# Moving the last step of a fused AdaLN-FFN block from VectorE to ScalarE and an accumulating DMA

## The chip, the cores and the metric

The kernel runs on one core of one Trainium2 chip. The metric is the device time of one execution in microseconds (us), lower is better. A core has five engines that matter here: TensorE (PE; its weight loads are shown as PEld) multiplies into PSUM, VectorE (DVE), ScalarE (ACT) and GpSimd (POOL) work elementwise, and SyncE (SP) issues DMAs. Each engine runs its own instructions in the order in which the program gives them. They wait for each other through semaphores.

## The reference

`x` has shape (64, 64, 512) in fp32: 64 samples b, 64 channels c, 512 positions t. Every sample chooses one of 200 matrices by its condition. Then comes a feed-forward block with two linear layers, 512 to 1024 to 512. Ahead of each layer the rows are passed through a Walsh-Hadamard transform (FWHT) and rounded to 8 bits with one scale a row; the weights are rounded to -1, 0, 1 times one scale. The result is added to `x`:

```python
def act_quant(x, bits):
    qb = float(2 ** (bits - 1) - 1)
    scale = qb / jnp.clip(jnp.max(jnp.abs(x), axis=-1, keepdims=True), EPS, None)
    q = jnp.clip(jnp.round(x * scale), -qb, qb) / scale
    return _ste(x, q)
def hbitlinear(x, w, bits):
    xq = act_quant(fwht(x), bits)
    wq = weight_quant(w)
    return jnp.einsum('bsd,fd->bsf', xq, wq)
...
w = weights[conditions]
y = jnp.einsum('bct,bcd->bdt', x, w)          # _L0_cond_ref
h = hbitlinear(y, w_up, ACT_BITS)
h = jnp.square(jax.nn.relu(h))
x = x + hbitlinear(h, w_down, ACT_BITS)
```

## The kernel before, in words

**Tiling.** The 64 samples are cut into 16 blocks of four samples (`NP` = 16), so 256 rows (`TOK`) of the feed-forward block; a half `s` of a block is 128 rows, one per partition. Weights are rounded once, transposed and kept in SBUF as bf16 (`wuT`, `wdT`).

**Stages of a block n.** Each is a helper, one for each engine that takes part:

- `load` (L108, SP) brings x with channels and halves of t on the partitions (`xc`); `gather` (L115) brings the four samples' matrices by four indirect DMAs from GpSimd's queue.
- `xbutterfly` (L196) does the first step of the FWHT on x, on GpSimd in the loop; `wsign` (L208, GpSimd) completes the matrices with a signed copy. `cond_pe` (L215) multiplies them, and `cond_act` (L226, ScalarE) copies the product out of PSUM.
- `h1_pe` (L236) does the rest of the first FWHT by a 128 x 128 Hadamard matrix, `h1_dve` (L246 to L251) takes the rows' maxima and the scales, `h1_act` (L256, L263) rounds, `h1_small` (L269, L271) prepares two factors, `t1` (L276) transposes by two DMAs from SP's queue.
- `up_pe` (L284) is the up-projection in two halves h, `up_act` (L294, L296) the relu and the square.
- `mix` (L196) does three butterfly stages of the second FWHT on VectorE, two instructions each; `h2_pe` (L326) the rest on TensorE, `h2_dve` (L335 to L339) the maxima and scales, `h2_act` (L256) and `t2_act` (L354) the rounding, and L356 the transposes, from SP's queue.
- `out_scale` (L361) makes the scale of the result, `osc`. `down_pe` (L366) is the down-projection of one half into one PSUM bank `po`. `down_dve` (L376) is one VectorE instruction that computes po times osc plus `xr`. `xr` is x once more, in the layout of the result, loaded by `load_residual` (L124, SP, one DMA of 512 KB a block). Then SP stores the half (L379, 256 KB).

**Order.** It is written out by hand in the loop `for k in range(NP + 3)` (L440). One turn works on five blocks at once: `up = k` is projected up, `ah = k + 2` goes through its first FWHT (and `ah + 1` through `cond`), `mx = k - 1` is mixed, `tr = k - 2` goes through its second FWHT, and `dn = k - 3` is projected down and stored. The down-projection thus first runs at k = 3. On every engine, and on SP's and GpSimd's DMA queues, the instructions follow in the order of the loop's text. So SP has in a turn: load of `xc` for block k + 4, load of `xr` for `tr`, the two transposes of `t2_act`, the store of half 0, the two transposes of `t1`, the store of half 1. GpSimd has: two butterflies and `wsign` for `ah + 1`, then four gathers for k + 4. In the last turns the upward stages fall away, and blocks 14 and 15 have their rounding and transposes by halves (L455, L471).

**Buffers.** The six PSUM banks of pool `ps` make three tiles used in turn by cond, h1, up and h2; pool `pso` has two banks for `po`. `xr` has two buffers, the result tile `ot` four of half a block.

Of the kernel before, what the change touches and what calls it, by code (L numbers as in the profile page):

```python
# [7 lines left out]
F32 = mybir.dt.float32  # L8
BF16 = mybir.dt.bfloat16
I32 = mybir.dt.int32  # L10
AF = mybir.ActivationFunctionType
ALU = mybir.AluOpType
# [3 lines left out]
P = 128  # L16
# [22 lines left out]
def adaln_ffn_kernel(  # L39
# [10 lines left out]
    nc = tc.nc  # L50
    B, C, T = x.shape
# [10 lines left out]

    xv = x.rearrange("(n s b) c t -> n (b c) s t", s=2, b=2)
    xcv = x.rearrange("(n b) c (a t) -> n (c a) b t", b=4, a=2)
    ov = out.rearrange("(n s b) c t -> n s (b c) t", s=2, b=2)
    cwv = cw.rearrange("s c d -> (s c) d")

    const = ctx.enter_context(tc.tile_pool(name="const", bufs=1))
# [1 line left out]
    work = ctx.enter_context(tc.tile_pool(name="work", bufs=2))  # L70
# [26 lines left out]
    idx = const.tile([P, B], I32, tag="idx")  # L97
    nc.vector.tensor_scalar(idx, cnd, float(C), row_f, ALU.mult, ALU.add)

    xc, xr, w2 = {}, {}, {}  # L100

    def load_hm():
        nc.sync.dma_start(hm, had)
# [1 line left out]
    def load(n):  # L105

        xc[n] = loads.tile([P, 4, T // 2], F32, tag="xc", name=f"xc_{n}")
        nc.sync.dma_start(xc[n], xcv[n])  # L108

    def gather(n):  # L110

        w2[n] = loads.tile([P, 4, P], F32, tag="w2", name=f"w2_{n}")
        for b in range(4):
            i = 4 * n + b
            nc.gpsimd.indirect_dma_start(  # L115
                out=w2[n][:, b, :D],
                out_offset=None,
                in_=cwv,
                in_offset=bass.IndirectOffsetOnAxis(ap=idx[:, i : i + 1], axis=0),
            )  # L120

    def load_residual(n):
        xr[n] = work.tile([P, 2, T], F32, tag="xr", name=f"xr_{n}")
        nc.sync.dma_start(xr[n], xv[n])  # L124


    wuT = const.tile([P, NJ, FF], BF16, tag="wuT")
# [64 lines left out]
    pz2, qs2, t2, r2, q2T, osc, po, ot = {}, {}, {}, {}, {}, {}, {}, {}  # L192
# [5 lines left out]
    def xbutterfly(n, engine="p"):  # L198

        xb[n] = work.tile([P, 4, 2, P], F32, tag="xb", name=f"xb_{n}")  # L200
        v = xc[n].rearrange("p b (j q) -> p b j q", j=2)
        e = nc.gpsimd if engine == "p" else nc.vector
        for i in range(2):
            butterfly(e, [xb[n][:, :, j] for j in range(2)], [v[:, :, j] for j in range(2)], i)

    def wsign(n):

        nc.gpsimd.tensor_scalar(w2[n][:, :, D:], w2[n][:, :, :D], sgn, 1.0, ALU.mult, ALU.mult)  # L208

    def cond_pe(n):  # L210

        py[n] = ps.tile([P, 4, 2, 2, D], F32, tag="ps", name=f"py_{n}")
        for b in range(4):
            for j in range(2):
                nc.tensor.matmul(  # L215
                    py[n][:, b, j].rearrange("p a d -> p (a d)"),
                    xb[n][:, b, j, :],
                    w2[n][:, b, :],
                    start=True,
                    stop=True,  # L220
                )

    def cond_act(n):

        yT[n] = work.tile([P, 4, 4, D], F32, tag="yT", name=f"yT_{n}")
        nc.scalar.copy(  # L226
            yT[n].rearrange("p c b d -> p b c d"), py[n].rearrange("p b j a d -> p b (j a) d")
        )
# [49 lines left out]
    def up_pe(n, h):  # L278

        ph[h] = ps.tile([P, NF // 2, TOK], F32, tag="ps", name=f"ph_{n}_{h}")  # L280
        for i in range(NF // 2):
            f = h * NF // 2 + i
            for j in range(NJ):
                nc.tensor.matmul(  # L284
                    ph[h][:, i],
                    wuT[:, j, f * P : (f + 1) * P],
                    qT[n][:, j, :],
                    start=(j == 0),
                    stop=(j == NJ - 1),
                )  # L290

    def up_act(n, h):

        nc.scalar.activation(ph[h], ph[h], AF.Relu)  # L294
        gf[n, h] = work.tile([P, NF // 2, TOK], F32, tag="gf", bufs=4, name=f"gf_{n}_{h}")
        nc.scalar.activation(gf[n, h], ph[h], AF.Square)  # L296
# [26 lines left out]
    def h2_pe(n, s):  # L323
        pz2[s] = ps.tile([P, NF, P], F32, tag="ps", name=f"pz2_{n}_{s}")
        for f in range(NF):
            nc.tensor.matmul(  # L326
                pz2[s][:, f, :], mixed[n, 2][:, f, s * P : (s + 1) * P], hm, start=True, stop=True
            )

    def h2_dve(n, s):  # L330
        if s == 0:
            t2[n] = small.tile([P, 2], F32, tag="t2", name=f"t2_{n}")
        am = small.tile([P, 1], F32, tag="am2", name=f"am2_{n}_{s}")
        flat = pz2[s].rearrange("p f q -> p (f q)")
        nc.vector.tensor_reduce(am, flat, AX.X, ALU.max, apply_absolute_value=True)  # L335
        t = t2[n][:, s : s + 1]
        nc.vector.tensor_scalar(t, am, 1.0 / QB, e2[n][:, s : s + 1], ALU.mult, ALU.max)  # L337
        qs2[s] = small.tile([P, 1], F32, tag="qs2", name=f"qs2_{n}_{s}")
        nc.vector.reciprocal(qs2[s], t)  # L339

    def h2_act(n, s):
        if s == 0:
            r2[n] = work.tile([P, 2, FF], F32, tag="r2", bufs=1, name=f"r2_{n}")
        quantize(r2[n][:, s], pz2[s].rearrange("p f q -> p (f q)"), qs2[s])
# [3 lines left out]
    def t2_act(n, s=None):  # L348

        if n not in q2T:  # L350
            q2[n] = work.tile([P, 2, FF], BF16, tag="q2", name=f"q2_{n}")
            q2T[n] = work.tile([P, NF, TOK], BF16, tag="q2T", name=f"q2T_{n}")
        sl = slice(0, 2) if s is None else slice(s, s + 1)
        nc.scalar.activation(q2[n][:, sl], r2[n][:, sl], AF.Copy, bias=-MAGIC)  # L354
        for i in range(2)[sl]:
            nc.sync.dma_start_transpose(q2T[n][:, :, i * P : (i + 1) * P], q2[n][:, i])  # L356
# [14 lines left out]
                stop=(f == NF - 1),  # L371
            )

    def down_dve(n, s):
        o = work.tile([P, T], F32, tag="ot", bufs=4, name=f"ot_{n}_{s}")
        nc.vector.scalar_tensor_tensor(  # L376
            o, po[s], osc[n][:, s : s + 1], xr[n][:, s], ALU.mult, ALU.add
        )
        nc.sync.dma_start(ov[n, s], o)  # L379

    ku = const.tile([P, 1], F32, tag="ku")
    ke = const.tile([P, 1], F32, tag="ke")
# [9 lines left out]
    def valid(n):  # L392
        return 0 <= n < NP
# [46 lines left out]
    for k in range(NP + 3):  # L440
        up, ah, tr, dn, mx = k, k + 2, k - 2, k - 3, k - 1
        if valid(k + 4):
            load(k + 4)
        if valid(tr):
            load_residual(tr)
        if valid(ah + 1):
            xbutterfly(ah + 1)
            wsign(ah + 1)
        if valid(k + 4):
            gather(k + 4)  # L450
        if valid(tr):
            h2_pe(tr, 0)
            h2_dve(tr, 0)
            h2_act(tr, 0)
            if tr >= NP - 2:  # L455
                t2_act(tr, 0)
        if valid(up):
            up_pe(up, 0)
        if valid(mx) and mx < NP - 1:
            mix(mx, 1, 0)  # L460
            mix(mx, 1, 1)
        if valid(up):
            up_act(up, 0)
        if k == 0:
            cond_pe(2)
            cond_act(2)
        if valid(tr):
            h2_pe(tr, 1)
            h2_dve(tr, 1)
            h2_act(tr, 1)  # L470
            if tr >= NP - 2:  # L471
                t2_act(tr, 1)
        if valid(up):
            up_pe(up, 1)
            up_act(up, 1)
        if valid(tr) and tr < NP - 2:
            t2_act(tr)
        if valid(mx) and mx < NP - 1:
            mix(mx, 2, 0)
        if valid(ah):  # L480
            h1_pe(ah)
            h1_dve(ah)
        if valid(mx) and mx < NP - 1:
            mix(mx, 2, 1)
        if mx == NP - 1:
            for s in range(2):
                for stage in (1, 2):
                    mix(mx, stage, 0, s)
                    mix(mx, stage, 1, s)
        if valid(dn):  # L490
            out_scale(dn)
            down_pe(dn, 0)
            down_dve(dn, 0)
        if valid(ah):
            h1_act(ah)
            t1(ah)
            h1_small(ah)
        if valid(up):
            mix(up, 0, 0)
            mix(up, 0, 1)  # L500
        if valid(ah + 1):
            cond_pe(ah + 1)
            cond_act(ah + 1)
        if valid(dn):
            down_pe(dn, 1)
            down_dve(dn, 1)
        if k == 0:
            for i in range(CH):
                weight_sum("down", i, "a")
        if k == 1:  # L510
            sd.append(weight_scale("down"))
            for i in range(2):
                weight_round("down", wdT, i)
                weight_clip("down", wdT, i)
        if k == 2:
            for i in range(2, CH):
                weight_round("down", wdT, i)
                weight_clip("down", wdT, i)
# [29 lines left out]
```

## Time and profile before

| | us |
|---|---|
| median of the three runs shown | 295.7 |
| lowest and highest of them | 294.04 and 297.8 |
| the profiled execution, whole time | 298.29 |
| the profiled execution, span from first to last instruction | 296.5 |
| TensorE busy, mean granted clock 0.954 | 246.7 (83%) |
| VectorE busy | 244.7 (83%) |
| ScalarE busy | 199.8 (67%) |
| GpSimd busy | 126.5 (43%) |
| DMA queue of SP, share of the 16 engines' time | 61.1% |
| DMA queue of GpSimd, share of the 16 engines' time | 3.8% |
| `down_dve`, L376, 32 instructions | 23.7, or 747 ns each |
| rounding from PSUM, L256, 32 of 512 columns | 20.2, or 685 ns each |
| store, issue to landing, 256 KB | 2.4 |
| residual load, issue to landing, 512 KB | 4.0, 5.5, 6.9 (least, median, most) |
| gather, GpSimd's time for one issue | 0.94 to 1.87, median 0.95 |

The profile is of one execution. A group is all instructions of one source line on one engine with the same operands; its busy time is the sum over them. "Idle before" is how long the engine stood still ahead of a group, and the arrow names what ended the wait. In the row of slices the span is cut into 40 equal parts and each digit is the busy share of one in tenths. TensorE's matmuls overlap, so that their start times say more than the busy sum. A DMA's issue on a queue is short; what is told as landing is the time until its data had arrived.

### The profile page before, as it was taken

The numbers are of one execution on the slowest core, as the hardware profiler recorded it, in microseconds if no ns is written. First come the engines' busy times: TensorE is split into PE (matmuls) and PEld (weight loads), VectorE is DVE, ScalarE is ACT, GpSimd is POOL, SyncE is SP. The second block draws the span as 40 slices with busy tenths as digits, with TensorE's granted clock in tenths as the row PEclk, the third lists the DMA queues.
The fourth block names the chain that finished last, engine by engine and source line by source line (L and its number), as shares of the span: only waits on it lengthen the run. The fifth ranks groups of instructions, "written<-read, shape, count | busy, mean of one in ns | idle before, by whom it ended". The sixth has DMA issues, their size and how long they took to land. (4 is left out here: it accounts for less than half of the span.)

```text
span 296.5 us, 4792 instructions
## 1 busy us (share of the span) xinstructions
PE 246.7 (83%) x1796; PEld 203.0 (68%) x1796; DVE 244.7 (83%) x331; ACT 199.8 (67%) x231; POOL 126.5 (43%) x111
## 2 busy tenths in 40 slices
PE   0064969493789999998999999999999998987954
PEld 0063959492767878786878787878887878756721
DVE  1446708879789999999999999999999999999942
ACT  1346186965968686858686868687868786665350
POOL 2787804894653737282809683737310000000000
PEclk9998677988979999999999999999999999999989
DMA  5944594327495867575666766668683748275973
GB/s 193 359 112 92 92 299 108 100 45 143 124 142 162 150 188 156 184 156 182 138 200 127 213 136 201 140 198 137 201 141 109 142 108 177 81 206 112 214 169 143
DMA packets 81206, 46.55 MB, mean 157 GB/s; under 512 B 62112, under 2 KB 70432, under 8 KB 81184
## 3 DMA queue, kind: packets, MB, share of 16 engines
q1 hardware_dynamic: 79136, 44.15, 61.1%
q0 software_dynamic: 2048, 2.10, 3.8%
q8 instruction: 14, 0.23, 0.3%
q14 instruction: 8, 0.07, 0.1%
HBM read 23.17 MB, written 8.39 MB: 106 GB/s over the span
## 5 line engine op out<-in xcount | busy, mean ns | idle before, releaser
L256 ACT ACTIVATE r<-pz,qs 128x512 f32<-128x512 f32 (+1 forms) x64 | 55.8, 899 | 67.6 <-DVE qs L339 47.2
L196 DVE TENSOR_TENSOR g<-g 128x1024 f32<-128x1024 f32 (+1 forms) x68 | 83.6, 1256 | 0.1
L115 POOL DMA_INDIRECT w<-in_L_cond_weights,idx x64 | 71.9, 1123 | 21.9 <-issue 16.6
L284 PE MATMUL ph<-qT,wuT 128*128 128x256 bf16 x512 | 64.4, 282 | 10.4 <-ACT r L256 10.3
L326 PE MATMUL pz<-hm,g 128*128 128x128 f32 x512 | 63.6, 277 | 2.1 <-DVE g L196 2.1
L284 PEld LDWEIGHTS <-wuT 128*128 128x128 bf16 x512 | 51.9, 101 | 19.5 <-issue 12.5
L366 PE MATMUL po<-wdT,q2T 128*128 128x512 bf16 x256 | 60.8, 385 | 5.2 <-DMA q2T<-q 5.2
L326 PEld LDWEIGHTS pz<-hm,g 128*128 128x128 f32 x512 | 61.5, 193 | 4.9 <-DVE g L196 2.3
L196 POOL TENSOR_TENSOR xb<-xc 128x512 f32<-128x512 f32 x26 | 34.6, 1353 | 65.8 <-DMA xc<-in_x 63.6
L366 PEld LDWEIGHTS <-q2T 128*128 128x128 bf16 x256 | 25.2, 99 | 31.3 <-DMA q2T<-q 5.9
L236 PE MATMUL pz<-hm,yT 128*128 128x128 f32 x256 | 36.4, 301 | 8.8 <-ACT yT L226 8.2
L196 DVE TENSOR_TENSOR g<-gf,gf 128x1024 f32<-128x1024 f32 x32 | 41.9, 1349 | 1.6 <-ACT gf L296 1.6
L236 PEld LDWEIGHTS pz<-hm,yT 128*128 128x128 f32 x256 | 33.5, 211 | 12.4 <-ACT yT L226 9.0
L215 PE MATMUL py<-w,xb 128*128 128x128 f32 x256 | 35.5, 298 | 5.1 <-issue 3.8
L215 PEld LDWEIGHTS py<-w,xb 128*128 128x128 f32 x256 | 34.7, 213 | 6.8 <-issue 3.9
L335 DVE TENSOR_REDUCE am<-pz 128x1 f32<-128x1024 f32 x32 | 38.9, 1215 | 0.4 <-PE pz L326 0.4
L296 ACT ACTIVATE gf<-ph 128x1024 f32<-128x1024 f32 x32 | 32.8, 1024 | 1.0
L294 ACT ACTIVATE ph<-ph 128x1024 f32<-128x1024 f32 x32 | 32.5, 1016 | 0.0
L246 DVE TENSOR_REDUCE am<-pz 128x2 f32<-128x1024 f32 x16 | 19.6, 1223 | 15.6 <-PE pz L236 15.6
L354 ACT ACTIVATE q<-r 128x2048 bf16<-128x2048 f32 (+1 forms) x18 | 30.9, 1714 | 0.1
L376 DVE SCALAR_TENSOR_TENSOR ot<-po,osc,xr 128x512 f32<-128x512 f32 x32 | 23.7, 747 | 7.7 <-PE po L366 6.3
L208 POOL TENSOR_SCALAR w<-w,sgn 128x256 f32<-128x256 f32 x16 | 20.1, 1255 | 1.3 <-DMA w<-in_L_cond_weights,idx 1.1
(46 smaller groups left out, 109.6 us busy)
## 6 DMA issues: line engine op xcount, KB each, us to landing
xc<-in_x SPq DMA_DIRECT2D x16, 512.0 KB, 11.0
xr<-in_x SPq DMA_DIRECT2D x16, 512.0 KB, 5.5
out<-ot SPq DMA_DIRECT2D x32, 256.0 KB, 2.4
raw_up<-in_L_ffn_w_up SPq DMA_DIRECT2D x4, 512.0 KB, 7.6
raw_down<-in_L_ffn_w_down SPq DMA_DIRECT2D x4, 512.0 KB
w<-in_L_cond_weights,idx POOLq DMA_INDIRECT x64, 3.6
qT<-q SPq DMA_TRANSPOSE x32, 3.1
q2T<-q SPq DMA_TRANSPOSE x32, 3.2
```

The source lines that it names most:

```text
L115: nc.gpsimd.indirect_dma_start(out=w2[n][:, b, :D], out_offset=None, in_=cwv, in_offset=bass.IndirectOffsetOnAxis(ap=idx[:, i : i + 1], ax ...
L196: engine.tensor_tensor(dst[i], src[0], src[1], (ALU.add, ALU.subtract)[i])
L215: nc.tensor.matmul(py[n][:, b, j].rearrange("p a d -> p (a d)"), xb[n][:, b, j, :], w2[n][:, b, :], start=True, stop=True,)
L236: nc.tensor.matmul(pz1[n][:, s, c * P : (c + 1) * P], y[:, j * 2 + a, s * P : (s + 1) * P], hm, start=True, stop=True,)
L256: nc.scalar.activation(r, pz, AF.Copy, bias=MAGIC, scale=qs)
L284: nc.tensor.matmul(ph[h][:, i], wuT[:, j, f * P : (f + 1) * P], qT[n][:, j, :], start=(j == 0), stop=(j == NJ - 1),)
L294: nc.scalar.activation(ph[h], ph[h], AF.Relu)
L296: nc.scalar.activation(gf[n, h], ph[h], AF.Square)
L326: nc.tensor.matmul(pz2[s][:, f, :], mixed[n, 2][:, f, s * P : (s + 1) * P], hm, start=True, stop=True)
L335: nc.vector.tensor_reduce(am, flat, AX.X, ALU.max, apply_absolute_value=True)
L354: nc.scalar.activation(q2[n][:, sl], r2[n][:, sl], AF.Copy, bias=-MAGIC)
L366: nc.tensor.matmul(po[s], q2T[n][:, f, s * P : (s + 1) * P], wdT[:, f, :], start=(f == 0), stop=(f == NF - 1),)
```

## The change

`down_dve` is replaced by `down_act` and `finish`, and the residual load goes. ScalarE now takes each half's sums from PSUM, multiplies them with `osc` and writes them into a result tile of a whole block (`ot`, two buffers). After both halves a DMA from GpSimd's queue reads x from HBM and adds it onto that tile in SBUF (`accum_op=ALU.add`). SP then stores the block in one DMA of 512 KB, with the layout of `ov` changed to match. `out_scale` stays on VectorE.

```diff
-    ov = out.rearrange("(n s b) c t -> n s (b c) t", s=2, b=2)
+    ov = out.rearrange("(n s b) c t -> n (b c) s t", s=2, b=2)
...
-    def load_residual(n):
-        xr[n] = work.tile([P, 2, T], F32, tag="xr", name=f"xr_{n}")
-        nc.sync.dma_start(xr[n], xv[n])
...
-    def down_dve(n, s):
-        o = work.tile([P, T], F32, tag="ot", bufs=4, name=f"ot_{n}_{s}")
-        nc.vector.scalar_tensor_tensor(
-            o, po[s], osc[n][:, s : s + 1], xr[n][:, s], ALU.mult, ALU.add
-        )
-        nc.sync.dma_start(ov[n, s], o)
+    def down_act(n, s):
+
+        if s == 0:
+            ot[n] = work.tile([P, 2, T], F32, tag="ot", name=f"ot_{n}")
+        nc.scalar.activation(ot[n][:, s], po[s], AF.Copy, scale=osc[n][:, s : s + 1])
+
+    def finish(n, s=None):
+
+        sl = slice(0, 2) if s is None else slice(s, s + 1)
+        nc.gpsimd.dma_start(ot[n][:, sl], xv[n][:, sl], accum_op=ALU.add)
+        nc.sync.dma_start(ov[n][:, sl], ot[n][:, sl])
...
-        if valid(tr):
-            load_residual(tr)
...
             down_pe(dn, 0)
-            down_dve(dn, 0)
+            down_act(dn, 0)
...
             down_pe(dn, 1)
-            down_dve(dn, 1)
+            down_act(dn, 1)
+            finish(dn)
```

In the loop the first half's step stands between `down_pe(dn, 0)` and `h1_act(ah)`, the second half's step and `finish` at the end of the turn, behind `cond_act(ah + 1)`.

More of the change, by code (lines that the diff above doesn't have):

```diff
@@ L98, in adaln_ffn_kernel @@
     nc.vector.tensor_scalar(idx, cnd, float(C), row_f, ALU.mult, ALU.add)
-    xc, xr, w2 = {}, {}, {}
+    xc, w2 = {}, {}
     def load_hm():
```

## The prediction

> **What bounds the kernel now.** I read the slices first, for where it is full. From the tenth slice (about 70 us) to the thirty-sixth both TensorE and VectorE stand at 8 or 9 tenths, ScalarE at 6 to 8.
>
> ```profile
> PE   0064969493789999998999999999999998987954
> DVE  1446708879789999999999999999999999999942
> ACT  1346186965968686858686868687868786665350
> ```
>
> Next the table of stretches, cut at the starts of the wide ScalarE rounding (L354), one a loop turn: stretch, length, then busy us of TensorE, its weight loads, VectorE, ScalarE, GpSimd, clock, DMA share, GB/s.
>
> ```profile
> 169.93:184.60 14.67, 14.52 (x114) 12.00 (x113) 14.05 (x18) 11.40 (x15) 8.45 (x8) 1.00 0.69 170
> 199.18:213.53 14.35, 14.35 (x114) 12.00 (x113) 13.66 (x20) 11.39 (x14) 7.68 (x8) 1.00 0.78 175
> 256.00:267.65 11.65, 10.65 (x82) 8.31 (x81) 11.42 (x16) 7.90 (x8) 0.00 (x0) 1.00 0.51 136
> ```
>
> Two engines are within some tenths of the length of a turn; ScalarE leaves about 3 us, GpSimd 6. Nine turns from 94.87 to 228.36 (k = 3 to 12) take 133.49, so 14.83 each. TensorE cannot go below the sum of its eight groups. Start to start in the timeline from 92.96: down 1.73, cond 1.78, down 1.73, h2 1.78, up 1.75, h2 1.78, up 1.75, h1 1.89: 14.19. So **a turn can lose 0.64 us at most**, however much VectorE work goes. The list of waits (total, times, longest) says the same: matmuls wait little, ScalarE waits for VectorE.
>
> ```profile
> ACT r L256 <- DVE qs L339: 47.2, 27, 5.5
> PE ph L284 <- ACT r L256: 10.3, 10, 4.6
> PEld pz L236 <- ACT gf L296: 3.4, 10, 0.3
> POOL xb L196 <- DMA xc<-in_x: 63.6, 10, 10.7
> ```
>
> Last the chain that ended last, for the end (start, us, what):
>
> ```profile
> 279.90 0.74 DVE ot L376
> 280.64 1.14 DVE am L335
> ...
> 284.56 3.06 DMA q2T<-q
> 287.61 0.04 issue
> 287.66 4.94 PE po L366 x16
> 292.60 0.03 issue
> 292.63 0.75 DVE ot L376
> ```
>
> After 267 there is no up-projection to fill TensorE: a chain in which VectorE, ScalarE, a transpose and the last stores follow each other.
>
> **What the Trainium skill says.** "ScalarE: Activation LUTs", What ACT_TABLE_LOAD costs: a [128,N] ACTIVATE with one pointer operand takes about 280 + 0.833 N ns, 706 at N = 512. The trace agrees: 685 ns for the 512-wide form of L256, also PSUM to SBUF with a scale from a tile. "DMA: Bandwidth & Descriptors", Anatomy of one DMA: about 2.0 us plus bytes over 436 GB/s for a GpSimd-issued one, an estimate of 3.2 us for 512 KB. The trace is above such figures: the 32 KB gathers land after 3.6 in the median, since the DMA engines are 60 to 70% busy. "SBUF — State Buffer", Who interferes with whom: a VectorE instruction with two SBUF inputs contends with a GpSimd one that reads SBUF. The trace agrees: the mix at 125.46 takes 2.17 us beside the x butterfly, its fellows 1.2.
>
> ```profile
> 124.04 2.51 POOL L196 TENSOR_TENSOR xb<-xc 128x512 f32<-128x512 f32 x2 [6.55 <-DMA xc<-in_x]
> 125.46 2.17 DVE L196 TENSOR_TENSOR g<-g 128x1024 f32<-128x1024 f32 x1
> ```
>
> **The change part by part.**
>
> *VectorE loses 32 passes* of 0.747 (L376), 23.9 us; two a turn, 1.5. It is a bound together with TensorE, so a turn gains only down to TensorE's 14.19. Reaching it needs the results in time: in the turn at 202.63 the maximum starts at 204.96, behind the second pass, though its sums are done at 204.58. So it comes 0.38 earlier, and the waits of L284 (about 0.2) and L236 (0.3) shrink.
>
> *ScalarE gets 32 evictions* of 0.685, some 0.65 each back to back, 1.3 a turn. The first lies ahead of h1_act, t1's operand and the copy out of cond; behind the second is the next turn's h2_act. What hides them is ScalarE's gap: it ends the copy at 204.60 and starts L256 at 206.71, 2.11 idle, which shrinks by 0.38 as said, so 0.43 stays over. Their readers are a turn away. Without that cover 1.3 us a turn would be paid. But the cover is thin, and the x butterfly will now fall on other mixes (below), which can put qs up to 1 us later. I take a turn of **14.4**, about a third of the way from 14.19 back to 14.83: 9 × 0.43 = **-3.9** (ends -5.8 and 0; beyond 0 is the ring rival).
>
> *The turns k = 14 and 15* have TensorE waits of 0.76 and 1.00 before L284 (250.34, 262.01), caused by VectorE. Both go: **-1.8** (ends -1.8 and 0). At k = 13 TensorE runs without a gap from 230.07 to 244.10: nothing to gain.
>
> *GpSimd gets 16 accumulating DMAs*, queued behind the gathers and ahead of the next x butterfly. GpSimd ran a turn ahead of TensorE until now (x butterfly at 212.16, its matmuls at 227 to 230); now it waits each turn for the second eviction. Count from h2's first matmul: eviction ends at 17.6 (copy out of cond ends 16.3 after it now, plus the two evictions of 1.3), then issue, butterfly, wsign, and the cond matmuls of the next turn at 14.4 + 10.8 = 25.2. So 7.6 us are there. Butterfly 2.5 to 3.5 and wsign 0.5 to 2.5 (mean 1.3) are in the trace; the issue is not. Its lower bound is a gather's 0.94, its upper twice the slowest gather, 3.7 (256 rows against 128). I take 1.8, as it falls beside the mixes, where gathers take 1.7 to 1.9: 1.8 + 3.0 + 1.3 = 6.1. Hidden, cost 0; cover 1.5.
>
> *SP loses 16 residual loads (0.55) and 16 of 32 store issues (0.53)* and gains a wait: each store waits for the accumulation to land. Behind it stand the next load of xc and the next transposes of q2. With issue to landing L = 6.5 the store goes out at about 17.6 + 6.5 - 14.4 = 9.7 into the next turn; the transposes are due at 12.8 and the butterfly wants xc a turn later. Hidden until L is about 9. L is not in the trace. The nearest row is the residual load it replaces, same bytes and rows: 4.0, 5.5, 6.9 (least, median, most). Bounds: 4.0, and 8.8 (6.9 plus a slow gather's issue of 1.87). I take 6.5 where it runs beside transposes, 5.5 at the end, alone.
>
> *The end.* VectorE loses the passes at 279.23 to 280.64 (and one at 270.06), so the last maxima come 2.2 earlier. But SP now holds the store of block 13 ahead of the transposes of block 15: the eviction of block 13 ends near 277.2, it lands at 283.7, the transpose goes at 284.3 against 284.56 before. What is left of the gain is about a microsecond from there and the warmer last matmuls (pitch 0.43 for the first half in the chain, 0.22 elsewhere): -1.6 (ends -2.4 and +1). The last pass of 0.75 becomes an eviction of 0.69: -0.1. New is the accumulation, +5.5 (4.0 to 8.8), and one store of 512 KB for one of 256: landing 2.4 before, 512 KB of xc 3.96 (issued 208.20, used 212.16), less some of that for issue: +1.0 (0.5 to 1.6). Together **+4.8**.
>
> *Nothing else*: the output layout is the same bytes; the loaded residual's buffer goes, and none waited for it.
>
> Sum: -3.9 - 1.8 + 4.8 = **-0.9**. The profiled execution takes 298.29 (span 296.5 and 1.8 around it), so 297.4; it stands 2.6 above the median of the runs shown, 295.7, so 294.8; I say **295**.
>
> **The rivals.**
> 1. *Gain and price cancel* (forecast, 0.50): as above, 290 to 301.5 by the ends of L and of the turn.
> 2. *TensorE's floor and a quick accumulation* (0.24): turns of 14.2 (-5.7), -1.8, L = 4.0 and the full -2.4 in the end (+2.1): -5.4, so 290.3. Two things lead below 289.8: in the turn of 14.35 TensorE still waits 0.27 by the timeline, so the floor may be 14.1 (-0.9 more), and L may be the page's 3.2 (-0.8): 288.6. For it: TensorE's waits are recorded, small and all behind VectorE's results. Against: it needs every term at its good end.
> 3. *The ring through GpSimd's queue* (0.26): eviction, DMA issue, butterfly, wsign, cond matmuls, eviction. A turn cannot be shorter than 17.6 - 10.8 = 6.8 plus the three on GpSimd. From 8.0 us there it is longer than now; with an issue of 3.7, butterfly 3.5, wsign 1.5 it is 8.7, a turn 15.5: 9 × 0.67 = +6.0, with -1.8 and +4.8 gives +9.0, 304.7. From 8.4 it is slower by over 2%. For it: the wait for xc that hides GpSimd's order now (63.6 us) is all the slack there is. Against: gathers mostly issue in 0.94. An L near 8.8 adds to it, twice in the end (SP's wait and the last accumulation): about +5.6.
> 4. *It doesn't relieve VectorE* because the butterfly stretches two mixes a turn instead of one: -0, so 298.7; inside the first case's range.
>
> **The numbers.** Two per cent is 5.9 us, about what a measurement of this kernel can tell from no change. Faster 0.24, within 0.50, slower 0.26. Range **287.5 to 306**: about one in ten beyond each end.
>
> **What would show it.** L376 gone, a 512-wide ScalarE group of some 0.65 to 0.7; turns of 14.2 to 14.6, TensorE's waits before L284 and L236 gone, ScalarE's wait for L339 about 1.3 a turn shorter; GpSimd waiting for ScalarE before its DMA; in the end, 5 to 6 us from last eviction to last store. Wrong if cond matmuls wait for GpSimd (rival 3), if the turn stays at 14.8, or if the last store follows at once.

## The result and the profile after

The changed kernel takes 318.27 us (median of four runs, 315.49 to 320.44), the kernel before 296.75 beside it: ratio 1.073, 95% interval 1.065 to 1.080. It is **slower by 7%**, 21.5 us, outside the range of 287.5 to 306. Medians here and below are of all runs, ratios and intervals only of those within 1.5% of the kernel's fastest run, and of e9's four runs below only two are.

The slices of the changed kernel, in the same 40 parts of a span now of 315.9 us:

```profile
PE   0064964948699899989997999899989999885060
DVE  1446549887777989798979897989798889883000
ACT  1345479758687499849984998599769987866010
POOL 2788809966602929692968297838711011103010
```

VectorE no longer stands at 9 throughout, and neither does TensorE: both go up and down, and GpSimd does so with a period of two turns. In the last slices TensorE and VectorE stand idle for long stretches. So there are two losses, and the starts of the wide rounding (L350 here) tell them apart. Stretches: length, busy TensorE, weight loads, VectorE, ScalarE, GpSimd, clock, DMA share, GB/s.

```profile
142.24:155.13 12.89, 12.44 (x98) 10.09 (x97) 11.67 (x14) 12.45 (x17) 7.07 (x7) 1.00 0.66 130
155.13:173.32 18.19, 16.35 (x131) 13.80 (x130) 16.34 (x20) 12.66 (x16) 14.41 (x11) 1.00 0.90 198
260.46:271.45 10.99, 10.31 (x80) 7.94 (x79) 10.03 (x13) 9.06 (x10) 1.18 (x1) 1.00 0.74 144
```

Short and long stretches alternate. The table counts the same four parts in both kernels and in those of the experiments below: up to the rounding of k = 3, ten turns from there to k = 13, two turns to k = 15, in which `cond` and then the first FWHT have fallen away, and the end.

| kernel | to k = 3 | ten turns | two turns | the end | span |
|---|---|---|---|---|---|
| before | 94.87 | 147.50 | 25.28 | 28.85 | 296.5 |
| after | 92.86 | 154.96 | 23.63 | 44.45 | 315.9 |
| difference | -2.0 | +7.5 | -1.7 | +15.6 | +19.4 |

The first part is ahead of any eviction. Its length goes with the granted clock there (0.87 before, 0.91 after; in all fourteen profiles from 90.6 us at 0.94 to 95.8 at 0.88) and says nothing of the change.

**The turns.** Timeline of the changed kernel in a long turn (start, us, engine, line, what, idle before):

```profile
162.29 1.32 POOL L379 DMA_DIRECT2D ot<-in_x  x1 [1.96 <-ACT ot L374]
162.55 5.83 DVE L192 TENSOR_TENSOR g<-g 128x1024 f32<-128x1024 f32 x2
163.11 3.05 POOL L192 TENSOR_TENSOR xb<-xc 128x512 f32<-128x512 f32 x2
165.58 3.06 POOL L204 TENSOR_SCALAR w<-w,sgn 128x256 f32<-128x256 f32 x1
168.31 1.21 DVE L331 TENSOR_REDUCE am<-pz 128x1 f32<-128x1024 f32 x1
```

The pair of mixes takes 5.83 us; in the short turns and before it takes 2.34. GpSimd waited for the eviction, issued its DMA, and now runs the butterfly and wsign exactly beside this pair. Behind it comes the maximum am, 3.5 us late, and with it the rounding on ScalarE and the PSUM tiles. Before, the pair ran alone and the butterfly fell on one lone mix (1.0 us more):

```profile
206.53 2.34 DVE L196 TENSOR_TENSOR g<-g 128x1024 f32<-128x1024 f32 x2
212.16 2.50 POOL L196 TENSOR_TENSOR xb<-xc 128x512 f32<-128x512 f32 x2 [5.60 <-DMA xc<-in_x]
213.56 2.17 DVE L196 TENSOR_TENSOR g<-g 128x1024 f32<-128x1024 f32 x1
```

In the changed kernel the pair is stretched in every second turn; why the turns alternate was not taken apart. The list of waits shows the tie: GpSimd waits for ScalarE where it waited for xc (total, times, longest).

```profile
POOL ot L379 <- ACT ot L374: 104.6, 15, 15.9
ACT r L252 <- DVE qs L335: 27.2, 11, 4.5
PEld L362 <- DMA q2T<-q: 15.3, 5, 10.2
```

**The end.** The same kernel's timeline, SP, GpSimd and the matmuls they hold up:

```profile
282.28 0.21 DVE L357 SCALAR_TENSOR_TENSOR osc<-t,scale_down,kd 128x2 f32<-128x2 f32 x1
282.58 1.27 ACT L374 ACTIVATE ot<-po,osc 128x512 f32<-128x512 f32 x2 [2.64 <-DVE osc L357]
...
285.02 1.20 POOL L379 DMA_DIRECT2D ot<-in_x  x1 [9.02 <-DMA out<-ot]
...
288.49 1.06 ACT L350 ACTIVATE q<-r 128x1024 bf16<-128x1024 f32 x1
...
291.33 0.37 SPq L380 DMA_DIRECT2D out<-ot  x1
291.87 5.89 SPq L352 DMA_TRANSPOSE q2T<-q  x2
...
299.40 5.48 PE L362 MATMUL po<-wdT,q2T 128*128 128x512 bf16 x16 [9.73 <-DMA q2T<-q]
...
305.90 1.18 POOL L379 DMA_DIRECT2D ot<-in_x  x1 [13.70 <-ACT ot L374]
311.54 0.37 SPq L380 DMA_DIRECT2D out<-ot  x1
```

Read from below: the last store goes 5.6 us after the last accumulation. The last down-projection waited for a transpose issued at 291.87, though its first operand was ready at 287.46 and its second at 289.55. SP had first to store block 13, whose accumulation landed at 291.3; that was issued at 285.02, late because block 13's scale stands behind eight mixes on VectorE (282.28). (From the end of the eviction to the issue 1.2 us pass, 0.3 for blocks 12, 14 and 15. The list names the store of block 12 for it, but e1, e2 and e5 have the same 1.2 without that wait, so the cause stays open.) The matmuls began 7.5 us after the first of these transposes was issued (3.1 before), beside that store and block 14's accumulation.

So the end falls into two halves. From the rounding of k = 15 to the last down-projection it is 28.0 us, 20.0 before; from there to the end of the span 16.5, 8.8 before. Each half loses 7.7 to 7.9 us. The scale's place was in the trace before, behind the same eight mixes:

```profile
278.92 0.22 DVE L361 SCALAR_TENSOR_TENSOR osc<-t,scale_down,kd 128x2 f32<-128x2 f32 x1
```

### The profile page after: what moved, and what is told of

Its sections match the earlier page's. It is cut to its first block, busy times and chain, and to the rows that moved or that the text cites. A ratio compares the mean times of both kernels' runs of the same rounds, so it can differ in the third digit from the quotient of the medians.

```text
span 315.9 us, 4752 instructions
## 1 busy us (share of the span) xinstructions
PE 243.3 (77%) x1796; PEld 200.0 (63%) x1796; DVE 232.7 (74%) x299; ACT 218.7 (69%) x263; POOL 157.9 (50%) x127
## 3 DMA queue, kind: packets, MB, share of 16 engines
q0 software_dynamic: 6400, 10.49, 20.2%
## 4 chain that ended last, share of the span: by engine, by line
DVE 30%; PE 25%; ACT 19%; issue 14%; DMA 4%; POOL 3%; POOLq 0%; ACTq 0%; DVEq 0%; SPq 0%
DVE g L192 16%; PE pz L322 7%; PE po L362 7%; DVE am L331 6%; ACT r L252 4%; PE pz L232 4%; PE py L211 4%; PE ph L280 4%; ACT q L259 3%; ACT yT L222 3%; DVE am L242 3%; POOL w L115 3%; DMA ot<-in_x 2%; ACT q L350 2%; ACT ph L290 1%
## 5 line engine op out<-in xcount | busy, mean ns | idle before, releaser
L192 DVE TENSOR_TENSOR g<-g 128x1024 f32<-128x1024 f32 (+1 forms) x68 | 99.3, 1486 | 0.1
L115 POOL DMA_INDIRECT w<-in_L_cond_weights,idx x64 | 76.6, 1197 | 22.3 <-issue 16.4
L379 POOL DMA_DIRECT2D ot<-in_x x16 | 20.3, 1267 | 113.6 <-ACT ot L374 104.6
L280 PE MATMUL ph<-qT,wuT 128*128 128x256 bf16 x512 | 62.6, 277 | 7.7 <-ACT r L252 7.6
L280 PEld LDWEIGHTS <-wuT 128*128 128x128 bf16 x512 | 50.9, 99 | 14.8 <-issue 8.3
L331 DVE TENSOR_REDUCE am<-pz 128x1 f32<-128x1024 f32 x32 | 39.1, 1221 | 15.1 <-PE pz L322 14.8
L192 POOL TENSOR_TENSOR xb<-xc 128x512 f32<-128x512 f32 x26 | 39.4, 1727 | 12.0 <-DMA xc<-in_x 11.9
L211 PEld LDWEIGHTS py<-w,xb 128*128 128x128 f32 x256 | 33.2, 208 | 18.2 <-issue 14.9
L192 DVE TENSOR_TENSOR g<-gf,gf 128x1024 f32<-128x1024 f32 x32 | 40.7, 1315 | 3.1 <-ACT gf L292 3.1
L232 PE MATMUL pz<-hm,yT 128*128 128x128 f32 x256 | 35.2, 296 | 8.2 <-ACT yT L222 8.2
L374 ACT ACTIVATE ot<-po,osc 128x512 f32<-128x512 f32 x32 | 21.4, 683 | 17.7 <-PE po L362 13.5
L204 POOL TENSOR_SCALAR w<-w,sgn 128x256 f32<-128x256 f32 x16 | 31.1, 1941 | 0.6 <-DMA w<-in_L_cond_weights,idx 0.6
L350 ACT ACTIVATE q<-r 128x2048 bf16<-128x2048 f32 (+1 forms) x18 | 30.9, 1715 | 0.1
```

The lines of the kernel that those rows point to most:

```text
L115: nc.gpsimd.indirect_dma_start(out=w2[n][:, b, :D], out_offset=None, in_=cwv, in_offset=bass.IndirectOffsetOnAxis(ap=idx[:, i : i + 1], ax ...
L192: engine.tensor_tensor(dst[i], src[0], src[1], (ALU.add, ALU.subtract)[i])
L211: nc.tensor.matmul(py[n][:, b, j].rearrange("p a d -> p (a d)"), xb[n][:, b, j, :], w2[n][:, b, :], start=True, stop=True,)
L232: nc.tensor.matmul(pz1[n][:, s, c * P : (c + 1) * P], y[:, j * 2 + a, s * P : (s + 1) * P], hm, start=True, stop=True,)
L280: nc.tensor.matmul(ph[h][:, i], wuT[:, j, f * P : (f + 1) * P], qT[n][:, j, :], start=(j == 0), stop=(j == NJ - 1),)
```

## The experiments

Two theories for the turns: the place in GpSimd's queue (1), or the evictions and the DMA's traffic as such (2). Two for the end: SP's wait ahead of the transposes (3), or accumulation and store one after the other (4). The parts in the table are from each run's profile, the ratios against the kernel before beside it. e1, e2, e3, e7 and e13 give the result tile a third buffer. No eviction of the changed kernel waits for a buffer, and e9 and e6, which mend one loss each, keep the two.

| kernel | ten turns | two turns | the end | median | ratio (95%) |
|---|---|---|---|---|---|
| before | 147.50 | 25.28 | 28.85 | 296 to 297 | 1 |
| after | 154.96 | 23.63 | 44.45 | 318.27 | 1.073 (1.065 to 1.080) |
| e2 accumulation late | 147.60 | 23.29 | 45.56 | 309.33 | 1.042 (1.034 to 1.050) |
| e9 filler on GpSimd | 144.05 | 23.30 | 44.65 | 306.13 | no interval |
| e1 store late | 154.63 | 23.64 | 37.96 | 309.61 | 1.043 (1.035 to 1.051) |
| e5 scale early | 150.81 | 23.43 | 41.30 | 312.35 | 1.052 (1.043 to 1.061) |
| e3 both late | 143.94 | 23.30 | 37.78 | 299.17 | 1.019 (1.010 to 1.028) |
| e6 old end | 154.87 | 23.62 | 29.55 | 302.38 | 1.026 (1.018 to 1.033) |
| e7 both late, old end | 145.08 | 23.30 | 28.31 | 292.19 | 0.990 (0.986 to 0.994) |
| e4 before, held | 142.63 | 25.21 | 31.25 | 294.65 | 0.993 (0.990 to 0.996) |
| e8 before, held longer | 142.87 | 25.21 | 33.05 | 297.37 | 1.007 (1.003 to 1.010) |
| e10 residual by GpSimd | 149.54 | 25.20 | 27.99 | 298.08 | 1.010 (1.006 to 1.014) |
| e12 before, held in the loop | 142.47 | 25.19 | 29.27 | 290.35 | 0.985 (0.975 to 0.996) |
| e13 e7 and held | 145.81 | 23.50 | 29.56 | 292.79 | 0.992 (0.989 to 0.995) |

**One part alone: GpSimd held (e4).** In the kernel before, at the end of `down_dve`:

```diff
+        if s == 1:
+            hold = small.tile([P, 1], F32, tag="hold", name=f"hold_{n}")
+            nc.gpsimd.tensor_copy(hold, o[:, :1])
```

> The kernel before with one part of the change alone: GpSimd gets a one-column copy of each block's second result half at the end of the turn, so it can't start the next butterfly of x ahead of time. ScalarE, VectorE's passes, loads and stores stay as before. Theory 1 (the order on GpSimd makes the turns longer, because the butterfly and wsign now fall beside the two-input mixes and hold them): turns go from 14.8 to about 15.5 and some mix pairs take 5 us or more instead of 2.3; time about +6 us, 302. Theory 2 (the evictions on ScalarE or the accumulating traffic make the turns longer): nothing changes, 296.

Neither. Turns became *shorter*, eight of the ten 14.19 to 14.20, TensorE's floor. Theory 1 as first put falls: to hold GpSimd back does no harm in itself. Here the butterfly starts beside the maximum, which reads PSUM alone, and only its second half meets the mixes (3.43 for the pair, 1.1 us more). Before, the lone mix lost 1.0, so it is not less stretching but its place that makes the turn shorter; which wait it takes away was not taken apart.

```profile
168.38 1.22 DVE L335 TENSOR_REDUCE am<-pz 128x1 f32<-128x1024 f32 x1
168.53 0.18 POOL L382 COPY hold<-ot 128x1 f32<-128x1 f32 x1 [3.15 <-DVE ot L376]
168.69 2.49 POOL L196 TENSOR_TENSOR xb<-xc 128x512 f32<-128x512 f32 x2
169.96 3.43 DVE L196 TENSOR_TENSOR g<-g 128x1024 f32<-128x1024 f32 x2
```

**The accumulating DMA behind the next turn's GpSimd work (e2).** The store goes with it, and both follow behind the loop for the last block.

```diff
         if valid(k + 4):
             gather(k + 4)
+        if valid(dn - 1):
+            accum(dn - 1)
+            store(dn - 1)
...
             down_act(dn, 1)
-            finish(dn)
```

> The changed kernel with the accumulating DMA and its store put behind the next turn's butterfly, wsign and gathers in GpSimd's queue, one more buffer for the result. Theory 1: GpSimd runs ahead again, mixes beside the butterfly cost 1 us and not 3.5, turns go from 15.5 to 14.2 to 14.6, time 8 to 11 us less than the changed kernel's, about 308, with the end as long as in the changed kernel. Theory 2: turns stay at 15.5, 318.

The time fell by 9, as theory 1 had it, though its turns came out at 14.8: the ten turns are back at 147.60, the end hardly touched. Every pair of mixes takes 2.34 again, and the butterfly falls elsewhere:

```profile
160.66 2.34 DVE L192 TENSOR_TENSOR g<-g 128x1024 f32<-128x1024 f32 x2
166.40 2.72 POOL L192 TENSOR_TENSOR xb<-xc 128x512 f32<-128x512 f32 x2
```

Evictions and traffic are all still there, so theory 2 falls.

**The hold made longer (e8).** As e4, and after the copy two writes (1.95 us):

```diff
             nc.gpsimd.tensor_copy(hold, o[:, :1])
+            fill = work.tile([P, 1024], F32, tag="fill", bufs=1, name=f"fill_{n}")
+            for _ in range(2):
+                nc.gpsimd.memset(fill, 0.0)
```

> The kernel before, held as in the one-column run, with two writes of zeros on GpSimd after the copy, some 1.8 us that read nothing from SBUF: they stand for the issue of the accumulating DMA and the later eviction. Nothing else of the change is there. Theory 1b (not the hold but its phase counts: if the butterfly starts after the first two mixes of a turn have started, they are held through butterfly and wsign): mix pairs of 5 us and more appear where the shorter hold had 3.4, turns go from 14.2 to 15 or more, time 302 to 308. Rival (the phase doesn't matter, and the loss in the changed kernel needs its evictions or its DMA): 294 to 297.

Missed: turns stay at 14.2, the pair at 3.42, although the butterfly starts 0.6 us after the mixes as in the long turn above. This time the butterfly was stretched (3.93) and wsign came clear of them, at 0.48:

```profile
160.28 3.42 DVE L196 TENSOR_TENSOR g<-g 128x1024 f32<-128x1024 f32 x2
160.90 3.93 POOL L196 TENSOR_TENSOR xb<-xc 128x512 f32<-128x512 f32 x2
164.81 0.48 POOL L208 TENSOR_SCALAR w<-w,sgn 128x256 f32<-128x256 f32 x1
```

So the start alone doesn't decide how much each of the two engines pays. What differs in the two traces is that in the long turn wsign runs beside the mixes too.

**The same delay in the changed kernel (e9).** In `finish`, behind the accumulating DMA, for blocks 0 to 8:

```diff
+        if n < 9:
+            fill = work.tile([P, 1024], F32, tag="fill", bufs=1, name=f"fill_{n}")
+            for _ in range(2):
+                nc.gpsimd.memset(fill, 0.0)
```

> The changed kernel with two writes of zeros on GpSimd (1.95 us, no reading of SBUF) between the accumulating DMA and the next butterfly, in the loop only. Theory 1c (the first two mixes of a turn and the butterfly meet with the butterfly ahead, and lose 3.5 us; what counts is where they meet): with 2 us more work on GpSimd the butterfly comes after these mixes, pairs of 5.8 us go, turns shorten from 15.5 to 14.5 or 15, time 4 to 8 us below the changed kernel's 318. Rival (GpSimd's queue is the bound, so each us put into it lengthens the ring): turns of 16.4 and more, 326.

The strongest of the runs: **2 us of useless work on GpSimd per turn made the changed kernel 12 us faster**, 10.9 of it in the ten turns by the two profiles, more than the 4 to 8 expected. They now take 14.41, TensorE's floor but for 0.2:

```profile
170.24 1.35 POOL L379 DMA_DIRECT2D ot<-in_x  x1
170.38 2.34 DVE L192 TENSOR_TENSOR g<-g 128x1024 f32<-128x1024 f32 x2
171.03 2.55 POOL L383 MEMSET fill<- 128x1024 f32 x2
173.54 3.48 POOL L192 TENSOR_TENSOR xb<-xc 128x512 f32<-128x512 f32 x2
177.00 0.48 POOL L204 TENSOR_SCALAR w<-w,sgn 128x256 f32<-128x256 f32 x1
```

Neither the DMA's issue nor the writes of zeros beside them stretch the mixes: 2.34. What stretched them was the butterfly with wsign, which now meets a lone mix for 0.5 us. The ring through GpSimd's queue as a sum of durations (the third rival) is not the bound either: with 2 us more in it the turn is shorter.

**The same queue without the change's other parts (e10).** The kernel before with e4's hold for blocks 0 to 8, and the residual of blocks 0 to 9 loaded behind it:

```diff
-        nc.sync.dma_start(xr[n], xv[n])
+        (nc.gpsimd if n < 10 else nc.sync).dma_start(xr[n], xv[n])
...
             down_dve(dn, 1)
+        if valid(tr) and tr < 10:
+            load_residual(tr)
```

> The kernel before with the residual of blocks 0 to 9 loaded by a plain DMA from GpSimd's queue at the end of the turn, behind the one-column copy that holds GpSimd there: the same 512 KB, the same issue on the same queue in the same place as the accumulating DMA, without the accumulation, without evictions on ScalarE, and with SP's stores as before. If a DMA of this size issued there is enough to stretch the mixes: pairs of 5 us and more, turns of 15 or above, 300 to 306. If it takes the evictions too (which move the turn's instants by a microsecond): turns of 14.2 to 14.4, 292 to 296.

In between: 298.08. The plain DMA takes GpSimd 0.75 us (the accumulating one 1.32), which puts the butterfly 0.5 us ahead of the mixes; the pair takes 4.20 and eight of the ten turns 14.96 to 14.98 (at clock 1.00), against 14.19 without it:

```profile
162.20 0.74 POOL L124 DMA_DIRECT2D xr<-in_x  x1
162.96 2.51 POOL L196 TENSOR_TENSOR xb<-xc 128x512 f32<-128x512 f32 x2
163.49 4.20 DVE L196 TENSOR_TENSOR g<-g 128x1024 f32<-128x1024 f32 x2
```

So a GpSimd DMA at this place costs through the butterfly's instant, evictions or not; that the full 5.83 needs the changed kernel's own instants was not tried further.

**SP freed (e1).** Store of a block at the end of the next turn, the last one behind the loop:

```diff
             down_act(dn, 1)
-            finish(dn)
+        if valid(dn - 1):
+            store(dn - 1)
+        if valid(dn):
+            accum(dn)
```

> The changed kernel with each block's store put at the end of the next turn in SP's queue, behind that turn's transposes, one more buffer for the result. Theory 3 (the end grows because SP waits for an accumulation ahead of the last transposes): the stretch from the last wide rounding to the end shrinks from 44 to about 35 us, turns stay near 15.5, time about 309. Theory 4 (the end grows because accumulation and store follow each other after the last eviction): it shrinks by 2 us at most, 316.

The end shrinks by 6.5 to 37.96, the turns do not move. That is less than theory 3 expected and more than theory 4 allowed: both hold, each for about half. The last transposes go at once now, and counted from the rounding of k = 15 the matmuls follow 7.6 us earlier than in the changed kernel, 0.3 later than before the change:

```profile
285.40 3.35 SPq L352 DMA_TRANSPOSE q2T<-q  x2
...
289.89 5.31 PE L362 MATMUL po<-wdT,q2T 128*128 128x512 bf16 x16 [2.67 <-DMA q2T<-q]
...
296.24 1.18 POOL L377 DMA_DIRECT2D ot<-in_x  x1 [6.12 <-ACT ot L374]
```

After it the accumulation still has to land and the store to follow, 11.3 us from its issue to the end of the span. From the last matmuls to the end it is 17.6 us, 8.8 more than before: that is theory 4's share.

**The scale ahead of the mixes (e5).**

```diff
+        if valid(dn):
+            out_scale(dn)
         if valid(ah + 1):
             xbutterfly(ah + 1)
...
-            out_scale(dn)
             down_pe(dn, 0)
```

> The changed kernel with the scale of the result computed at the head of the turn on VectorE instead of behind the mixes. Theory 3a (block 13 is evicted late because its scale stands behind the last eight mixes on VectorE, and SP's wait passes this on): the eviction of block 13 starts 3 to 4 us earlier, 279 instead of 282.6 in the changed kernel's count, and the end shortens by 3 to 4 us, about 314.5. Rival (GpSimd's accumulation of block 13 waited 9 us for the store of block 12, so the scale doesn't matter): less than 1.5 us.

The end shrinks by 3.15, and the time by 6, since the turns moved too (15.08). The size was as expected, the path was not:

```profile
278.56 1.06 ACT L350 ACTIVATE q<-r 128x1024 bf16<-128x1024 f32 x1
279.52 1.41 ACT L374 ACTIVATE ot<-po,osc 128x512 f32<-128x512 f32 x2
282.10 1.20 POOL L379 DMA_DIRECT2D ot<-in_x  x1 [7.75 <-issue]
...
290.01 0.37 SPq L380 DMA_DIRECT2D out<-ot  x1
290.55 3.04 SPq L352 DMA_TRANSPOSE q2T<-q  x2
...
294.35 1.20 POOL L379 DMA_DIRECT2D ot<-in_x  x1 [11.05 <-ACT ot L374]
294.39 5.74 PE L362 MATMUL po<-wdT,q2T 128*128 128x512 bf16 x16 [1.07 <-DMA q2T<-q]
```

The eviction of block 13 starts only 1.4 us earlier against the rounding of k = 15 (269.80), not 3 to 4: it now stands behind the rounding of block 14 on ScalarE. And from the issue of its accumulation to the store 7.9 us pass, 6.3 in the changed kernel, so that store and transposes go no earlier at all (20.2 us after that rounding, 19.9 in the changed kernel). What became shorter is the step behind: the matmuls start 3.8 us after the transposes are issued, not 7.5. Here block 14's accumulation goes out behind these transposes and not ahead of them.

**Both cures (e3), the old end (e6), both (e7).** e3 has `accum(dn - 1)` where e2 has it and `store(dn - 1)` where e1 has it. e6 has, with `OLDN` = 12 and the residual load back for the blocks from 12 on (e7 the same in e3):

```diff
-            down_act(dn, 1)
-            finish(dn)
+            (down_act if dn < OLDN else down_dve)(dn, 1)
+            if dn < OLDN:
+                finish(dn)
```

> The changed kernel with both cures: the accumulating DMA behind the next turn's work of GpSimd, and the store at the end of the next turn in SP's queue. If the two causes are separate, their gains add: 318.3 less 9 less 9, about 300 to 302, turns near 14.8, the end near 38. If they overlap: 306 or more.

> The changed kernel with blocks 12 to 15 done as before (residual load, pass on VectorE, stores by halves), the loop up to block 11 as changed. If the end costs 15 us and the loop 6: the end shrinks to about 29, time 302 to 304. If part of the loss in the end comes from the loop's state when it is entered: 307 or more.

> Both cures in the loop and blocks 12 to 15 as before. What is left of the change is the move of 24 passes from VectorE to ScalarE with an accumulation that nobody waits for. The prediction's turn of 14.4 would give 296.4 less 5.7, about 291. If TensorE[...] set the turn anyway: 14.8 a turn, 295 to 297.

In e7 blocks 12 to 15 go through a residual load and the VectorE pass again. The causes are separate: e3 is 19 below the changed kernel, 9 + 9 and a little; e6 has the end of the kernel before (29.55) and the turns of the changed one (15.49). With both mended (e7), what is left of the change makes 292.19, 1% *faster* than before. It fell between its two expectations: the ten turns take 14.5, and single ones still up to 15.5. Nothing there fixes where the butterfly falls, which is the likely reason, not a tested one.

**The best (e12) and a last combination (e13).** e12 is e4 with the hold for blocks 0 to 8 only (`if s == 1 and n < 9`); e13 is e7 with another hold:

```diff
             cond_act(ah + 1)
+            if valid(ah + 2):
+                hold = small.tile([P, 1], F32, tag="hold", name=f"hold_{k}")
+                nc.gpsimd.tensor_copy(hold, yT[ah + 1][:, 0, 0, :1])
```

> The kernel before with the one-column hold for blocks 0 to 8 alone, where a butterfly follows. In the run with all 16 holds the turns were 14.2 but the span ended 6.1 us after the last GpSimd instruction, against 3.1 us after VectorE's last one before. If a late GpSimd instruction lengthens the end: 3 us less than that run, about 291.5, ratio 0.983. If not: 294.5, ratio 0.993.

> The changed kernel with both cures and the old last four blocks (292.2 before), and GpSimd held for each butterfly until the copy out of cond by a one-column copy of it. If the hold gives turns of 14.2 here too, as it did without the change: 9 turns times 0.35 less, about 289. If the change's evictions spoil the phase: 292 or more. Beside the held kernel without the change this says what the eviction on ScalarE is worth once GpSimd is in place: 2 us (turns 14 and 15) or nothing.

e12 has the lowest median of all, **290.35, ratio 0.985**, and it has nothing of the change: VectorE keeps its passes. (Its interval takes in those of e7 and e13, so the order of these three is open.) Two turns of it:

```profile
149.08:163.27 14.19, 14.14 (x115) 12.10 (x115) 13.89 (x19) 11.39 (x14) 9.96 (x9) 1.00 0.72 177
163.27:177.47 14.20, 14.15 (x115) 12.11 (x115) 13.90 (x19) 11.40 (x15) 9.97 (x9) 1.00 0.67 176
```

TensorE is busy for all but 0.05 us of each, with VectorE at 13.9. In e13 the hold didn't lock the phase: turns of 13 and of 15.5 to 17 alternate, and the first expectation failed. So the evictions bring 1.7 to 1.9 us in the two turns to k = 15 (e13 and e7 against e12). In the ten turns no kernel with them got below the 142.47 that one tiny copy brings; what they would give with the butterfly held as in e12, e13 leaves open.

## Why the prediction was wrong, point by point

- **TensorE's floor of 14.19** as the most that a turn can give: right; e4 and e12 run at it.
- **VectorE's and ScalarE's parts** (a turn of 14.4, -3.9): the sum holds where the butterfly is out of the way. e9, with every part of the change in place, has 14.41. The eviction measured 683 ns against 685 taken. In the changed kernel itself the ten turns gained nothing and lost 7.5.
- **The failed step of the turns** is "I take 1.8 ... 1.8 + 3.0 + 1.3 = 6.1. Hidden, cost 0; cover 1.5", together with the price it gave the moved butterfly, "which can put qs up to 1 us later". It asked whether GpSimd has enough time, and it has. The 1 us came from the one lone mix that the butterfly met before. In the new place it meets a pair, with wsign behind it: 3.5 us in every second turn, at the head of the chain of am, scale and rounding. The Trainium skill's page "SBUF — State Buffer" has the direction in the section that the prediction names; in Summary: rules for kernel authors it says more, that of a VectorE instruction with two SBUF inputs and a GpSimd one that reads SBUF "the second one to issue **fully blocks** until the first finishes". From this rule and the times alone, 2.5 for the butterfly and 0.5 for wsign, my estimate for a mix behind both is 3.0 us. The runs agree with the direction; the 3.5 is above the estimate, and which of the two blocks they don't settle (e8 against the long turn). 1.3 for wsign was a mean over very different cases: 0.48 alone, up to 3.06 beside mixes.
- **Turns 14 and 15**, -1.8: measured -1.7, and TensorE's two waits before the up-projection are gone.
- **The end**, +4.8 predicted, +15.6 measured. Its single prices were good: issue to landing of the accumulation 6.8 in the median and 5.6 at the end (taken: 6.5 and 5.5), landing of the 512 KB store 3.0 against 2.4. The failed step is "the eviction of block 13 ends near 277.2, it lands at 283.7, the transpose goes at 284.3". It followed block 13's matmuls and passed over a wait: its scale stands behind the eight last mixes in VectorE's order. The eviction ended at 283.85, it landed at 291.3, the transpose went at 291.87 and the matmuls waited 7.5 for it. Counted from the rounding of k = 15 the matmuls came 8.2 us later than these steps give with the wait of 3.1 that the trace before had: 2.9 until the eviction's end (1.3 of it is the scale's place, by e5; the rest block 13's own matmuls, which ended later), 0.9 between eviction and landing, and 4.4, the largest, because the transposes took 7.5 and not 3.1, a term that the prediction took over unchanged. Behind the matmuls its sum was nearly right: +6.4 forecast, +7.7 measured. The warmer last matmuls did not come (5.48 us, 4.94 before). e1 shows that SP's wait is worth 7.6 us at the last matmuls and 6.5 of the 15.6 in the end; e5 that an earlier scale alone sends the transposes no earlier; e6 that all of it goes with the old last four blocks.
- **The rivals.** The second's floor is reached without the change (e4, e12), but its quick accumulation of 4.0 is not seen: 5.6 at the end, 6.8 in the median. The third named the right queue and the right side, and its mechanism, a ring of durations, is refuted by e9. Its sign, `cond`'s matmuls waiting, is there (1.84 us at 171.55), but they start 0.1 us after the late rounding ends (170.34, 1.11 us), not behind wsign, which ended at 168.6. "Twice in the end (SP's wait and the last accumulation)" was right in kind, but was put on a long landing, not on the order of the queues. The fourth named what happened in the turns, the butterfly on two mixes instead of one, and priced it at no more than the gain; it was 3.5 us.

## What to carry to other kernels

When a step is moved onto a queue, ask which instructions behind it start later and beside what they will then run, not only whether they still fit; where two engines hold each other up, as VectorE and GpSimd did here (2.34 us became 5.83), the phase of a loop can count for more than its sums. A wait on a DMA queue is paid by what stands behind it: put a store that waits for another DMA behind the transposes that others wait for, and give the last blocks, where nothing covers a landing, the path with the fewest DMAs in series. When turns alternate in length, look for two engines meeting; here a one-column copy that fixes an instant did as much for the ten turns (e12) as taking 1.5 us a turn off an engine (e3, e9).

## What the runs showed of the hardware that was not expected

- More work on GpSimd made the loop faster (e9, -12 us), and a hold on it as well (e12, -1.5%).
- A late GpSimd instruction lengthened the end of this kernel: with holds up to the last block the span ends 6.1 us after GpSimd's last instruction (e4: 284.05 to 290.2; e8: 290.33 to 296.4), against 3.1 us after VectorE's last one before. With the hold in the loop only (e12) it ends 3.2 us after VectorE's last one and has 2 us less in its end than e4. What takes these 6 us the traces don't show.
- An accumulating DMA of 512 KB took GpSimd 1.2 to 1.4 us to issue, a plain one of the same size and layout 0.75 (e10).
- Matmuls started 7.5 us (e9: 7.1) after the issue of transposes with a 512 KB store and an accumulation just ahead of them; where the store alone was ahead and the accumulation behind, 3.7 (e2) and 3.8 (e5); before 3.1.
